# The first microseconds of a four-layer convolution stack: weight kernels loaded ahead of the input frames, weights computed while the frames arrive, and layer 1's weights made later

## The chip, the core and the metric

The kernel runs on one core of one Trainium2 chip. The metric is the device time of one launch in microseconds (us). The core has five engines with a queue of instructions each: PE (TensorE, the matmuls), DVE (VectorE), ACT (ScalarE), POOL (GpSimd) and SP (SyncE, which here only issues DMAs). An engine takes its queue in order, so an instruction that waits holds up all behind it. ACT also issues some DMAs; such an issue stands in ACT's queue like any other instruction (it is shown as ACTq, those of SP as SPq).

## What is computed

An image batch `x` of 4 x 16 x 512 x 512 floats goes through four layers, each `x = x + conv(gn(x))` with a group norm of 8 groups. What the change touches is layer 0, cut to what matters:

```python
def _denoise_block(x, w1, b1, w2, b2, w3, b3, a, b, c):
    trip = _triplets(x)                       # each frame with its two neighbours
    o = a * conv(trip, w1, b1, dil 1) + b * conv(trip, w2, b2, dil 2) + c * conv(trip, w3, b3, dil 4)
    return tanh(o)
...
y = _denoise_block(x, blk1...)                # 16 frames per image
z = _denoise_block(y, blk2...)
...
x = x + _L0_conv_ref(_gn(x), ...)
```

Layer 1 is a 3 x 3 convolution with integer weights, layer 2 a box blur, layer 3 a convolution in the Fourier domain. Layer 1's weights are brought into their layout during layer 0, and that step is moved too.

## The kernel before, in words

Layer 0 (class `Layer0`, L121) takes the frames of an image in groups of four. Each group passes through six **slots** (`slot`, L668): in slot `(n, p)` PE computes tile `p` of group `n`, 14 x 16 matmuls into one of two PSUM tiles (`products`, L513, the matmul at L525). The six tiles of a group use six combinations `v` of the frames, in the order `ORDER = (1, 2, 3, 4, 0, 5)`, each with its own weight tile `w[q]`. I call the tiles of the first group m0 to m5.

What goes into the combinations: a raw frame is scaled and shifted on ACT (`normalised`, L377 and the two edge copies L378 and L379), transposed on DVE (L405), and gets its upper and lower rims from a second small tile `ek`, made the same way from a `rim` load that serves four frames (`rims`, L382). The scale and the shift come from the group norm: `bn_stats` of each half of a frame on DVE (`frame_stats`, L266), one aggregation for two frames (L268), a sum across partitions on POOL and a square root on ACT (`finish_stats`, L229, and `rstd_bias`, L806, the root at L812). DVE then forms the combinations (`early`, `late`; L441 is the shared helper `stt`), and after a tile is done ACT or DVE takes it out of PSUM (`gather`, L536).

The order is written out by hand (`manual_schedule`): `run` first calls `first` (L270), then the slots from group -1 on, and each engine's queue holds its instructions in the order in which the Python calls made them. `first` does, in this order:

- twelve loads of half frames (frames 0 to 5 of image 0, `HELD = 6`, L202) on SP;
- `layer1_weights` (L867): two loads on ACT, a memset (L876) and six products (L881) on DVE, and the store of the result on ACT (L882);
- `frame_stats` of frames 0 and 1;
- `weights` (L153): loads of the parameters `l0_par` (L159) and of the expanded kernels `l0_t` (L161), both on ACT, the weighted sums and their combinations on DVE (L163 to L178), and two stores of the result to a scratch in DRAM on ACT (L181);
- `load_weights` (L194) for each of the six `q`: four loads of 32 partitions each from that scratch into `w[q]`, on ACT (L196), 24 in all;
- twenty rim loads (two rim tiles, L202) on SP;
- `frame_stats` of frames 2 to 5, then `finish_stats` for the first three channel groups.

The slots of group -1 make the five frames that the first group needs first (0, 1, 3, 2, 4, in this order) and its first two combinations. `rest_of_first` (L297) runs at the end of each early slot: it loads and measures frames 6 to 15, two per turn, and in slot (-1, 3) calls `take_biases` (L183: two small loads on ACT, six small operations on DVE). Later, `load_weights` is called in a slot whenever the next tile belongs to the other convolution.

DMAs are numbered onto eight completion semaphores in turn, whichever engine issues them. A DMA that would reuse a semaphore whose earlier DMA is still out waits on its issuing engine until that DMA has landed. In the order of before, loads on SP thus wait for loads and stores that ACT issued.

Of the kernel before, what the change touches and what calls it, by code (L numbers as in the profile page):

```python
# [13 lines left out]
F32 = mybir.dt.float32  # L14
AF = mybir.ActivationFunctionType
# [5 lines left out]
P = 128  # L21
# [7 lines left out]
PX = 32  # L29
# [8 lines left out]
HELD = 6  # L38
# [12 lines left out]
def shape_constants():  # L51
# [57 lines left out]
    k["c_lc"] = (v[g].reshape(P, NYB, 8).transpose(1, 0, 2)[..., None] * of).reshape(NYB, P, P)  # L109
    row = np.zeros((P, 2, n))  # L110
    row[g == 3, 0] = fold(first)
    row[g == 3, 1] = -fold(hk)
    k["c_bias_row"] = row
# [3 lines left out]
def scratch(pool, name, shape):  # L117
    return pool.tile(shape, F32, tag=name, name=name)


class Layer0:  # L121
# [12 lines left out]
    def __init__(self, k, ctx, x1):  # L134
        self.k, self.tc, self.nc, self.a, self.x1 = k, k.tc, k.nc, k.a, x1
        tc = self.tc
        self.pools = {}
        for name, bufs in (("frames", 1), ("w", 1), ("sum", 1), ("ra", 2), ("rb", 2), ("x", 6), ("ek", 1)):
            self.pools[name] = ctx.enter_context(tc.tile_pool(name=f"l0{name}", bufs=bufs))
        self.psum = ctx.enter_context(tc.tile_pool(name="l0ps", bufs=2, space=PSUM))  # L140
        self.mv = k.stats.tile([P, NBG, 2], F32, name="mv1")
        self.top = k.stats.tile([P, B, C, 2], F32, name="top1")
        self.low = k.stats.tile([P, B, C, 2], F32, name="low1")
        self.frame_is = k.load(k.stats, "c_frame_is")
        self.parity = k.load(k.stats, "c_parity")
        self.free = [
            self.pools["frames"].tile([P, KN], F32, name=f"frame{i}", tag=f"frame{i}") for i in range(NFRAMES)
        ]
        self.todo, self.gn = {}, {}
        self.marks, self.moves = [], None  # L150


    def weights(self):  # L153

        k, nc = self.k, self.nc
        n = NPB * PX // 2
        self.w_dram = scratch(k.dram, "l0w", [2, PX, NQ, 2 * n])
        par = k.small.tile([P, 6], F32, name="l0par", tag="l0par")
        nc.scalar.dma_start(par, self.a["l0_par"])  # L159
        t = self.free[0][:, 0 : 9 * n].rearrange("p (d n) -> p d n", d=3)  # L160
        nc.scalar.dma_start(t, self.a["l0_t"].rearrange("p (d n) -> p d n", d=3))  # L161
        sums = self.free[1][:, 0 : 3 * n]
        nc.vector.tensor_scalar_mul(sums, t[:, 0], par[:, 3:4])  # L163
        for d in (1, 2):
            self.stt(sums, t[:, d], par[:, 3 + d : 4 + d], sums)
        c = [sums[:, i * n : i * n + n] for i in range(3)]
        s, u = (self.free[1][:, i * n : i * n + n] for i in (3, 4))
        wq = self.free[2][:, 0 : NQ * n].rearrange("p (q n) -> p q n", q=NQ)
        nc.vector.tensor_add(s, c[0], c[2])
        for q, op in ((1, ALU.add), (2, ALU.subtract)):  # L170
            nc.vector.tensor_tensor(wq[:, q], s, c[1], op)
        nc.vector.tensor_scalar_mul(wq[:, 1:3], wq[:, 1:3], -1.0 / 6.0)
        nc.vector.tensor_scalar_mul(u, c[2], 1.0 / 6.0)
        self.stt(u, c[0], 1.0 / 24.0, u)
        for q, f in ((3, 1.0 / 12.0), (4, -1.0 / 12.0)):
            self.stt(wq[:, q], c[1], f, u)
        nc.vector.tensor_scalar_mul(wq[:, 0], c[0], 0.25)
        nc.vector.tensor_copy(wq[:, 5], c[2])  # L178
        to = self.w_dram.rearrange("b p q (e n) -> e (b p) q n", e=2)
        for half in range(2):  # L180
            nc.scalar.dma_start(to[half], wq[2 * PX * half : 2 * PX * half + 2 * PX])  # L181
# [10 lines left out]
                self.stt(o, par[:, d : d + 1], par[:, 3 + d : 4 + d], o)  # L192

    def load_weights(self, conv, q):  # L194
        for i in range(4):
            self.nc.scalar.dma_start(self.w[q][PX * i : PX * i + PX], self.w_dram[conv, :, q])  # L196


    def move(self, to, src, what="loads"):
# [70 lines left out]
    def first(self):  # L270

        self.mv0 = self.k.stats.tile([P, G, 2], F32, name="xmv0")
        self.held = {}
        for t in range(HELD):
            fr = self.free.pop()
            raws = [fr[:, 2 * W * h : 2 * W * h + 2 * W] for h in range(2)]
            for h in range(2):
                self.load_half(raws[h], 0, t, h)
            self.held[0, t] = fr, raws
        self.k.layer1_weights(self.free[3])  # L280
        for t in range(2):
            self.frame_stats(t, self.held[0, t][1])
        self.weights()
        for q in ORDER:
            self.load_weights(0, q)
        self.rims_ahead = {t0: self.load_rims(0, t0) for t0 in (0, 1)}
        for t in range(2, HELD):
            self.frame_stats(t, self.held[0, t][1])
        self.free.append(self.held.pop((0, HELD - 1))[0])
        self.finish_stats(0, self.mv0[:, 0 : HELD // 2])  # L290
        self.ahead = []

    def load_ahead(self, t):
# [3 lines left out]
    def rest_of_first(self, n, p):  # L297

        if (n, p) == (-1, 0):
            for t in (HELD, HELD + 1):  # L300
                self.load_ahead(t)
        if (n, p) == (-1, 3):
            self.take_biases()
        for _ in range(2 if (n, p) in ((-1, 5), (0, 0)) else 1 if n >= 0 else 0):
            if self.ahead:
                t, raws = self.ahead.pop(0)
                self.frame_stats(t, raws)
                self.load_ahead(t + 2)
                for lo, hi in ((2, 5), (5, G)):
                    if t == 2 * hi - 1:  # L310
                        self.finish_stats(0, self.mv0[:, lo:hi], lo)
# [67 lines left out]
        nc.scalar.copy(xp[:, :, W + 8 : W + 16], xp[:, :, W + 6 : W - 2 : -1])  # L379
        return xp.rearrange("p s (k j) -> p k s j", j=16)  # L380

    def rims(self, b, t0, raw):  # L382
        nc, k = self.nc, self.k
        ss = []
        for n in range(2):
            t = k.small.tile([P, 4], F32, name=f"rs_{b}_{t0}_{n}", tag="rs")
            nc.vector.tensor_mul(t, self.frame_is, self.gn[b][n][:, t0 : t0 + 4])
            o = k.small.tile([P, 1], F32, name=f"ro_{b}_{t0}_{n}", tag=f"ro{n}")
            nc.vector.tensor_reduce(o, t, AX.X, ALU.add)
            ss.append(o)  # L390
        xp = self.normalised(raw, ss[0], ss[1], f"r{b}_{t0}")
        ek = self.pools["ek"].tile([P, 33, PX], F32, name=f"ek_{b}_{t0}", tag="ek")
        nc.vector.transpose(ek, xp)
        return ek
# [392 lines left out]
class Kernel:  # L787
# [79 lines left out]
    def layer1_weights(self, t):  # L867

        nc = self.nc
        self.l1_wt = scratch(self.dram, "l1_wt", [P, 2, 4, 2, C])  # L870
        w = t[:, 0 : 9 * C].rearrange("p (h d c) -> p h d c", h=3, d=3)
        row = t[:, 9 * C : 9 * C + 2]
        wt = t[:, 256 : 256 + 16 * C].rearrange("p (a n y c) -> p a n y c", a=2, n=4, y=2)
        nc.scalar.dma_start(w, self.a["l1_w"])
        nc.scalar.dma_start(row, self.a["c_pair"])
        nc.vector.memset(wt, 0.0)  # L876
        for a, yo, dhs in ((0, 0, (0, 1)), (0, 1, (None, 0)), (1, 0, (2, None)), (1, 1, (1, 2))):
            o = wt[:, a, 0:3, yo, :]
            for y, d in enumerate(dhs):
                if d is not None:  # L880
                    nc.vector.scalar_tensor_tensor(o, w[:, d], row[:, y : y + 1], o, ALU.mult, ALU.add)  # L881
        nc.scalar.dma_start(self.l1_wt, wt)  # L882
# [176 lines left out]
    def layer2(self, x2, x3, sums, gn, l3):  # L1059
        tc, nc = self.tc, self.nc  # L1060
        res, under_way = [], []
        with ExitStack() as ctx:
# [87 lines left out]
            with tc.manual_schedule():  # L1150
                for i in range(3):
                    load(i)
                normal(0)
                first(0)
                normal(1)
                for i in range(n + 1):
                    if i + 3 < n:
                        load(i + 3)
                    if i + 1 < n:
                        first(i + 1)  # L1160
                    if i + 2 < n:
                        normal(i + 2)
                    if i > 0:
                        column_sums(i - 1)
                    if i < n:
                        second(i)
                    advance()
                    if i > C and i % C == 1 or i == n:
                        b = (i - 1) // C - (i < n)
                        res.append(self.group_stats(gps, self.stats, f"x3_{b}", mv[:, b], G))  # L1170
                        if b == 1:
                            under_way.append(self.edges(l3, 0, res, sums, tiles, *eps))
# [547 lines left out]
```

## Time and profile before

| | us |
|---|---|
| median of 3 runs | 5329.93 |
| lowest, highest of these | 5324.8, 5330.24 |
| the profiled execution | 5314.9 |
| its span, first to last instruction | 5313.1 |
| ACT busy in it | 2491.1 (47%) |
| POOL busy in it | 6.8 (0%) |
| share of PE, DVE and DMA in the chain that ended last | 89%, 6% and 2% |

The granted clock of TensorE was 0.982 over the span. The profile is one execution; its durations are sums and means over that one. A row of its timeline gives the start in us, the duration (for merged rows that of the whole stretch), the engine, the line, the operation, what it writes and reads, how many instructions were merged, and in brackets how long the engine had been idle before it and what ended that. A row with SPq or ACTq is a DMA issue, not the transfer. A row of the waits gives who waited for what, the sum in us, how many times, and the longest.

### The profile page before, as it was taken

What the parts mean: (1) busy time and instruction counts of PE and PEld (TensorE: products, weight loads), DVE (VectorE), ACT (ScalarE), POOL (GpSimd) and SP (SyncE); (2) the same over time, 40 slices, a digit from 0 to 9 for tenths busy, and PEclk for the clock granted to TensorE, in tenths of its full rate; (3) what the DMA queues carried; (4) which work ended last, traced back from release to release, by engine and by line L of the source; (5) the groups of instructions that cost most, each with busy time, mean ns of one, the idle gap of its engine ahead of it and who ended that gap; (6) DMA issues with size and microseconds to landing.
All of it is one profiled execution on the core that took longest, in us unless ns stands there. A gap on an engine that the chain in (4) does not pass through costs nothing.

```text
span 5313.1 us, 270477 instructions
## 1 busy us (share of the span) xinstructions
PE 5014.8 (94%) x125040; PEld 3651.4 (69%) x125040; DVE 4034.6 (76%) x4764; ACT 2491.1 (47%) x3954; POOL 6.8 (0%) x20
## 2 busy tenths in 40 slices
PE   4999998999999999989999789998999989999999
PEld 3676676766776856758766655566887867777776
DVE  7867989768988669987689855555555578888887
ACT  2543445533255533444122445554454446666665
POOL 0000000000000000000000000000000000000000
PEclk9999999999999999999999999999999989999999
DMA  5555554555545455543346377776666655555554
GB/s 170 170 145 157 144 156 148 161 148 137 143 152 169 139 160 137 150 134 117 103 128 153 126 222 231 234 238 202 225 222 199 214 158 143 144 149 148 143 143 121
DMA packets 445356, 861.49 MB, mean 162 GB/s; under 512 B 74304, under 2 KB 96704, under 8 KB 443968
## 3 DMA queue, kind: packets, MB, share of 16 engines
q1 hardware_dynamic: 415792, 797.68, 51.8%
q10 hardware_dynamic: 28432, 46.52, 2.7%
q8 instruction: 979, 16.04, 1.4%
q14 instruction: 153, 1.25, 0.1%
HBM read 503.87 MB, written 340.03 MB: 159 GB/s over the span
## 4 chain that ended last, share of the span: by engine, by line
PE 89%; DVE 6%; issue 2%; DMA 2%; ACT 1%; SPq 0%; ACTq 0%; POOL 0%; DVEq 0%; POOLq 0%
PE m L525 51%; PE l1p L975 10%; PE l2p L1082 8%; PE u L1550 4%; PE s L1491 4%; PE u L1491 4%; PE u L1513 2%; PE pt L1525 2%; DVE l2o L1122 2%; PE l2p L1133 1%; DVE st L1123 1%; DVE frame L441 0%; PE pr L1535 0%; ACT xp L377 0%; DVE zr L627 0%
## 5 line engine op out<-in xcount | busy, mean ns | idle before, releaser
L525 PE MATMUL m<-frame,l0w 32*32 32x512 f32 x86016 | 2856.1, 604 | 170.5 <-DVE frame L481 74.4
L525 PEld LDWEIGHTS m<-frame,l0w 32*32 32x32 f32 x86016 | 2073.7, 103 | 952.0 <-issue 363.1
L441 DVE SCALAR_TENSOR_TENSOR frame<-frame,frame 128x2376 f32<-128x2376 f32 x232 | 607.9, 2629 | 9.2 <-DMA xs<-in_x 0.8
L975 PE MATMUL l1p<-l1q,l_wt 32*32 32x512 f32 x12288 | 482.6, 600 | 61.3 <-DVE l1q L965 35.7
L975 PEld LDWEIGHTS l1p<-l1q,l_wt 32*32 32x32 f32 x12288 | 258.3, 103 | 231.6 <-issue 155.4
L1122 DVE TENSOR_TENSOR l2o<-l2x,l2p 128x512 f32<-128x512 f32 x256 | 172.7, 675 | 270.4 <-PE l2p L1082 270.4
L652 ACT ACTIVATE junk<-xb,neg 128x1024 f32<-128x1024 f32 x256 | 294.2, 1149 | 62.1 <-DMA l0w<-l0w 32.9
L1082 PEld LDWEIGHTS l2p<-k_c_band,l2y 128*128 128x128 f32 x2048 | 256.8, 190 | 76.0 <-issue 55.2
L1082 PE MATMUL l2p<-k_c_band,l2y 128*128 128x144 f32 (+1 forms) x2048 | 284.3, 292 | 6.1
L1082 PE MATMUL l2p<-k_c_band,l2n 128*128 128x144 f32 (+1 forms) x2048 | 272.5, 294 | 14.4 <-ACT l2n L1100 10.9
L1111 ACT COPY l2y<-l2p 128x512 f32<-128x512 f32 x256 | 149.9, 586 | 286.9 <-PE l2p L1082 286.9
L1082 PEld LDWEIGHTS l2p<-k_c_band,l2n 128*128 128x128 f32 x2048 | 265.8, 199 | 15.3 <-ACT l2n L1100 11.4
L992 DVE BATCH_NORM_STATS2 l1st<-l1o 128x6 f32<-128x512 f32 x256 | 158.2, 681 | 140.3 <-ACT l1o L990 140.3
L990 ACT ACTIVATE l1o<-l1p,k_l_bias,l_osc 128x1024 f32<-128x1024 f32 x128 | 147.2, 1201 | 240.1 <-PE l1p L975 234.2
L1550 PE MATMUL u<-k_c_hil,zt 128*128 128x128 f32 x2048 | 255.9, 278 | 0.0
L558 ACT COPY C<-m 128x1024 f32<-128x1024 f32 x64 | 61.6, 1014 | 405.9 <-PE m L525 317.6
L1550 PEld LDWEIGHTS u<-k_c_hil,zt 128*128 128x128 f32 x2048 | 238.4, 192 | 2.1 <-issue 0.8
L405 DVE STREAM_TRANSPOSE frame<-xp 128x1056 f32<-128x1056 f32 x128 | 162.8, 1282 | 90.5 <-ACT xp L379 90.4
L1526 ACT COPY zt<-pt 128x512 f32<-128x512 f32 x256 | 131.4, 599 | 207.8 <-PE pt L1525 207.8
L1456 DVE TENSOR_TENSOR xc<-l3n,k_c_tab 128x2048 f32<-128x2048 f32 x64 | 146.7, 2292 | 108.1 <-ACT l3n L1440 108.1
L1569 DVE SCALAR_TENSOR_TENSOR l3o<-u,l3t 128x256 f32<-128x256 f32 x512 | 192.3, 427 | 22.3 <-ACT l3t L1561 19.5
L975 PE MATMUL l1p<-l1x,l_wt 32*32 32x512 f32 x4088 | 196.7, 597 | 0.0
(309 smaller groups left out, 6376.9 us busy)
## 6 DMA issues: line engine op xcount, KB each, us to landing
y<-y SPq DMA_DIRECT2D x256, 264.0 KB
frame<-y SPq DMA_DIRECT2D x512, 132.0 KB
x<-l1o SPq DMA_DIRECT2D x256, 256.0 KB
l2x<-x SPq DMA_DIRECT2D x64, 1024.0 KB
x<-l2o SPq DMA_DIRECT2D x64, 1024.0 KB
l3x<-x SPq DMA_DIRECT2D x256, 256.0 KB
out<-l3o SPq DMA_DIRECT2D x256, 256.0 KB
l1x<-x SPq DMA_DIRECT2D x252, 256.0 KB
```

What stands on the lines that cost most here:

```text
L405: nc.vector.transpose(v[:, :, 4 + h : 68 : 2], xp)
L441: self.nc.vector.scalar_tensor_tensor(o, x, f, y, ALU.mult, ALU.add)
L525: ins = nc.tensor.matmul(ps[PX * j : PX * j + PX, i, :].rearrange("p (k r) -> p k r", r=64), w[rows, n], v[rows, k0 : k0 + 8, r0 : r0 + 64 ...
L652: nc.scalar.activation(junk, xs[h], f, bias=neg, accum_out=self.out_sums[n][:, 2 * t + h : 2 * t + h + 1])
L975: ins = nc.tensor.matmul(ps[32 * j : 32 * j + 32, b, :], wt[rows, a, d], qs[v % 3][rows, k, d : d + W] if d < 3 else raws[v][rows, k], sta ...
L992: nc.vector.bn_stats(st[b][:, u, :], o[:, b, :])
L1082: nc.tensor.matmul(ps[:, lo:hi], lhs[:, k, at : at + P], band[:, j : j + hi - lo], start=(k == 0), stop=(k == 3), skip_group_check=True,)
L1111: nc.scalar.copy(yts[i][:, wb, :], ps)
L1122: nc.vector.tensor_add(o[:, hb, :], xt[:, hb, :], ps)
L1491: nc.tensor.matmul(ps[b][32 * j : 32 * j + 32], f[rows, n, j, :], x[rows, j, :], start=(i == 0), stop=(i == 2 and tag == "s"), skip_group_ ...
L1550: nc.tensor.matmul(po[:, bass.ts(k, P)], zt[:, b, k ^ 1, :], hil[:, k, :], start=False, stop=(k == 3), skip_group_check=True,)
L1569: nc.vector.scalar_tensor_tensor(o[:, v].rearrange("p k u -> p u k"), po[:, HW:W].rearrange("p (u k) -> p u k", u=2), s, t.rearrange("p (u ...
```

## The change

It has six parts, all in `first` or in the slots up to (0, 1).

1. `weights` becomes a generator in two halves. The first half is called ahead of the frame loads: it issues the loads of `l0_par` and `l0_t`, now on SP, in front of the twelve frame loads. The second half, the DVE work and the two stores (still on ACT), is called directly after the frame loads, ahead of all `frame_stats`.
2. A one-element `Sqrt` on ACT, with a memset of its input on DVE, stands at the start. ACT's first table load is placed ahead of it.
3. The 24 loads of `load_weights` in `first` go to SP (`queue`, chosen by whether `now` is still None), behind the twenty rim loads. Later calls, in slots, stay on ACT.
4. The `frame_stats` of all six frames follow each other. The scales of the two rim tiles (`rim_scale`, four small DVE operations each, cut out of `rims`) are computed together right after `finish_stats`, where before the second four stood between the transposes of frames.
5. `take_biases` moves from slot (-1, 3) to (-1, 5): on ACT and on DVE it now stands behind frame 4 instead of ahead of frame 2.
6. `layer1_weights` becomes a generator too. Its two loads go to SP in slot (-1, 1); its memset, its six products and its store (on ACT) are done in slot (0, 1), in a tile of its own, ahead of that slot's `bn_stats`.

The operations, their shapes and their number are otherwise unchanged: DVE gets one instruction more (a memset of one column), ACT one activation more, and 28 DMA issues move from ACT to SP. In the built program f11, the last half-frame load on SP, waits for the semaphore of the first weight store, and the second rim load waits for that of the second store. From slot (0, 2) on the two programs stand in the same order on every engine and use the same semaphores.

```diff
     def weights(self):
...
-        nc.scalar.dma_start(par, self.a["l0_par"])
+        nc.sync.dma_start(par, self.a["l0_par"])
         t = self.free[0][:, 0 : 9 * n].rearrange("p (d n) -> p d n", d=3)
-        nc.scalar.dma_start(t, self.a["l0_t"].rearrange("p (d n) -> p d n", d=3))
+        nc.sync.dma_start(t, self.a["l0_t"].rearrange("p (d n) -> p d n", d=3))
+
+        warm = k.small.tile([P, 1], F32, name="warm", tag="l0warm")
+        nc.vector.memset(warm, 1.0)
+        nc.scalar.activation(warm, warm, AF.Sqrt)
+        yield
         sums = self.free[1][:, 0 : 3 * n]
...
     def load_weights(self, conv, q):
+        queue = self.nc.sync if self.now is None else self.nc.scalar
         for i in range(4):
-            self.nc.scalar.dma_start(self.w[q][PX * i : PX * i + PX], self.w_dram[conv, :, q])
+            queue.dma_start(self.w[q][PX * i : PX * i + PX], self.w_dram[conv, :, q])
...
         self.held = {}
+        weights = self.weights()
+        next(weights)
         for t in range(HELD):
             fr = self.free.pop()
             raws = [fr[:, 2 * W * h : 2 * W * h + 2 * W] for h in range(2)]
             for h in range(2):
                 self.load_half(raws[h], 0, t, h)
             self.held[0, t] = fr, raws
-        self.k.layer1_weights(self.free[3])
-        for t in range(2):
-            self.frame_stats(t, self.held[0, t][1])
-        self.weights()
+        next(weights, None)
+        self.rims_ahead = {t0: self.load_rims(0, t0) for t0 in (0, 1)}
         for q in ORDER:
             self.load_weights(0, q)
-        self.rims_ahead = {t0: self.load_rims(0, t0) for t0 in (0, 1)}
-        for t in range(2, HELD):
+        for t in range(HELD):
             self.frame_stats(t, self.held[0, t][1])
         self.free.append(self.held.pop((0, HELD - 1))[0])
         self.finish_stats(0, self.mv0[:, 0 : HELD // 2])
+        self.rim_scales = {t0: self.rim_scale(0, t0) for t0 in (0, 1)}
...
-        if (n, p) == (-1, 3):
+        if (n, p) == (-1, 5):
             self.take_biases()
+        if (n, p) == (-1, 1):
+            self.l1w = self.k.layer1_weights(self.pools["sum"].tile([P, 1024], F32, name="l1w_make", tag="E"))
+            next(self.l1w)
+        if (n, p) == (0, 1):
+            next(self.l1w, None)
...
+    def rims(self, b, t0, raw):
+        nc = self.nc
+        ss = (self.rim_scales.pop(t0) if b == 0 and t0 < 2 else None) or self.rim_scale(b, t0)
         xp = self.normalised(raw, ss[0], ss[1], f"r{b}_{t0}")
...
-        nc.scalar.dma_start(w, self.a["l1_w"])
-        nc.scalar.dma_start(row, self.a["c_pair"])
+        nc.sync.dma_start(w, self.a["l1_w"])
+        nc.sync.dma_start(row, self.a["c_pair"])
+        yield
         nc.vector.memset(wt, 0.0)
```

More of the change, by code (lines that the diff above doesn't have):

```diff
@@ L149, in __init__ @@
         self.todo, self.gn = {}, {}
-        self.marks, self.moves = [], None
+        self.marks, self.moves, self.now = [], None, None
     def weights(self):
@@ L380, in normalised, with rim_scale @@
         return xp.rearrange("p s (k j) -> p k s j", j=16)
-    def rims(self, b, t0, raw):
+    def rim_scale(self, b, t0):
         nc, k = self.nc, self.k
@@ L390, in rims @@
             ss.append(o)
+        return ss
+    def rims(self, b, t0, raw):
+        nc = self.nc
+        ss = (self.rim_scales.pop(t0) if b == 0 and t0 < 2 else None) or self.rim_scale(b, t0)
         xp = self.normalised(raw, ss[0], ss[1], f"r{b}_{t0}")
```

## The prediction

> **What bounds the kernel now.** I read the page first. PE is busy for 94% of the span and leads the chain that ended last with 89%; the first of its 40 slices is the exception, with a 4:
>
> ```profile
> PE 5014.8 (94%) x125040; PEld 3651.4 (69%) x125040; DVE 4034.6 (76%) x4764; ACT 2491.1 (47%) x3954; POOL 6.8 (0%) x20
> PE   4999998999999999989999789998999989999999
> ```
>
> So the beginning, in which PE has nothing to do, is added in full to what follows. The timeline of the first 200 us shows what the beginning consists of (start, duration, engine, line):
>
> ```profile
> 6.14 1.29 DVE L266 BATCH_NORM_STATS2 xst<-frame 128x6 f32<-128x512 f32 x2 [1.53 <-DMA frame<-in_x]
> 8.41 1.29 DVE L266 BATCH_NORM_STATS2 xst<-frame 128x6 f32<-128x512 f32 x2 [0.98 <-DMA frame<-in_x]
> ...
> 18.03 0.57 DVE L163 TENSOR_SCALAR frame<-frame,l0par 128x672 f32<-128x672 f32 x1 [4.11 <-DMA frame<-in_l_t]
> ...
> 23.72 4.84 DVE L266 BATCH_NORM_STATS2 xst<-frame 128x6 f32<-128x512 f32 x8
> 23.84 1.25 ACTq L181 DMA_DIRECT2D l0w<-frame  x2
> ...
> 29.14 14.32 ACTq L196 DMA_DIRECT2D l0w<-l0w  x24
> ...
> 34.10 0.17 DVE L242 COPY xmp<-xmv 128x3 f32<-128x3 f32 x1
> ...
> 36.34 0.17 DVE L810 TENSOR_SCALAR v_x<-var 128x3 f32<-128x3 f32 x1
> 43.50 1.28 ACT L812 ACT_TABLE_LOAD   x1 [43.50 <-DMA l0w<-l0w]
> 44.80 0.20 ACT L812 ACTIVATE s_x<-v_x 128x3 f32<-128x3 f32 x1
> ...
> 47.02 1.24 ACT L377 ACTIVATE xp_r<-rim,ro,ro 128x1024 f32<-128x1024 f32 x1 [2.02 <-DVE ro L389]
> ...
> 53.42 1.24 ACT L377 ACTIVATE xp_r<-rim,ro,ro 128x1024 f32<-128x1024 f32 x1 [1.44 <-DVE ro L389]
> ...
> 74.38 46.38 PE L525 MATMUL m<-frame,l0w 32*32 32x512 f32 x1344 [74.38 <-DVE frame L481]
> ```
>
> Three things are to be seen. DVE waits 4.11 us for the kernels `l0_t`, issued at 5.72 and landed 12.25 us later beside the frames. The variance is ready at 36.51 (36.34 + 0.17), but ACT is issuing 24 loads until 43.5 and then loads a table, so the root starts at 44.80: 8.3 us late. And ACT waits 1.44 us before the second rim tile.
>
> PE waits twice more soon after; the timeline from 118 to 160 us:
>
> ```profile
> 119.95 2.63 DVE L441 SCALAR_TENSOR_TENSOR frame<-frame,frame 128x2376 f32<-128x2376 f32 x1
> ...
> 122.68 29.44 PE L525 MATMUL m<-frame,l0w 32*32 32x512 f32 x896 [1.93 <-issue]
> ...
> 153.31 7.26 PE L525 MATMUL m<-frame,l0w 32*32 32x512 f32 x213 [1.18 <-issue]
> ```
>
> The view names no releaser, but m3 starts 0.10 us after DVE ends its combination (122.58), and m5 0.10 us after DVE has taken the last piece of m3 out of PSUM (153.21). By the table of stretches DVE is busy for 42.38 of the 46.39 us under m0 to m2 and for 32.10 of the next 32.54. **So DVE, not PE, sets the pace from 75 to 153 us**: a start of m0 that is earlier than DVE can follow is given back at m3.
>
> The waits of SP's queue up to 50 us show a fourth thing, the shared completion semaphores:
>
> ```profile
> SPq L202 <- DMA l0w<-l0w: 9.3, 6, 5.4
> ```
>
> Loads on SP stand still for DMAs of another kind.
>
> **The change part by part.**
>
> *Kernels ahead of frames (part 1).* SP issues its three constants until 2.06, `l0_par` takes 0.66 (its row on ACT), so `l0_t` is issued at about 2.75. When does it land? Nearest row: the first frame half, 512 KB, was issued at 2.10 and used at 6.14, 4.0 us. `l0_t` has 1008 KB; the further 0.51 MB at 285 to 420 GB/s (the rates of the slices from 3 to 13 us) take 1.2 to 1.8 us. That gives 8.0 to 8.6; I take 8.2. Here the Trainium skill speaks against the change: "DMA: Bandwidth & Descriptors", section "Issuing engines are not separate DMA queues", says that DMAs run on the same 16 engines and interleave, whichever engine started them, and that another queue saves only issue time. Read so, `l0_t` shares with the frames as it did before, takes its 12.25 us again and lands at 15.0. But the rows show frames that stood in SP's one queue landing one after the other (6.14, 8.41), not together; ahead in that queue `l0_t` should land first. I go by the row; the rule's 15.0 is a rival.
>
> DVE's weights took 23.72 - 18.03 = 5.69 us, so they end at 13.9. Then all six frames' statistics: two frames took 28.88 - 23.72 = 5.16 and 34.10 - 28.88 = 5.22, so six take 15.5, to 29.4. (The first two, and `layer1_weights`, were hidden under the wait for `l0_t`; now these 5.2 us are in the open, and are counted.) From there to the scales: the same steps later in the trace, with no table and a free ACT, take 94.69 to 98.64 = 3.95, and the first rim scale 47.02 - 46.37 = 0.65. **The first `xp_r` starts at 34.0 instead of 47.02: 13.0 us earlier.**
>
> *Root's table (part 2).* Its 1.28 us goes to the wait for data at the start: inside the 13.0. The skill's "ScalarE: Activation LUTs", section "What ACT_TABLE_LOAD costs", counts 2.66 with a drain; here the root started 0.02 us after the load's end, so nothing beyond 1.28 was to be had. By the page the first `xp_r` would start 14.4 us earlier.
>
> *Loads back on SP (part 3).* What covers them? f11, the last half-frame, waits for the first weight store. The stores are issued at 14.0 to 14.6. Before, both landed at 29.0, 5.2 us after the first issue, with the frames nearly done; now frames are in flight, so at worst they behave like `l0_t` did before (12.25 us). From both ends they land at 19.2 to 26.8; I take 23, since the frames drain on the way. f11 then lands at about 25 and DVE wants it at 27.8. Of the rims ten issues at 0.62 us follow: first tile issued at 29.2, landed at 32.6 (a rim load took 3.41 in the chain); wanted at 34.0. Second tile at 38.8; wanted at 34.0 + 51.98 - 47.02 = 39.0. Close, but covered; at the worst end it is 3.6 us late. Then 24 weight loads at 0.43: SP is free at 46, the first weights landed at 40; m0 wants them at 59. Frames 6 and 7 come after that, in use from 65. Without this cover they'd cost 10.3.
>
> *Rim scales (part 4).* The 1.44 us wait goes; the second pair's 0.62 lies under ACT's `xp_r`. Gain 1.44.
>
> *Biases (part 5).* They lay from 65.32 to 66.48 ahead of frame 2's transposes: m0 gains 1.16. But DVE does them before m3 either way: net nothing there. Their loads now wait on ACT behind frame 4 (about 56); behind them on SP, frames 8 and 9 are wanted only at 75.
>
> *Layer 1's weights (part 6).* Memset 0.27 and six products 1.42 now stand in DVE's full stretch before m3: about 1.7 us lost, in full. Bounds: 0 if they fell into ACT's waits there (1.65 and 0.2 at 108 to 112), 2 with queueing; the order puts them after those waits, so 1.7. ACT's store waits for them, ahead of frame 6's and 7's making; ACT has idle time there (4.5 us), so nothing.
>
> *Sum.* m0 starts at 74.38 - 13.0 - 1.44 - 1.16 = 58.8. m3 starts at 122.68 - 13.0 - 1.44 + 1.7 = 109.9, while m2 ends at 58.8 + 46.4 = 105.2: PE's wait there grows from 1.93 to 4.7. From there both programs stand alike, so all later events shift together by **12.7 us**. The profiled execution, 5314.9 with 1.8 outside its span, would be 5302.2. The median of the runs, 15.0 above that execution for reasons that the profile doesn't show, gives 5329.93 - 12.7 = 5317.2.
>
> **The rivals.**
>
> *`l0_t` shares with the frames.* For: it took 12.25 us before, and eight loads are soon in flight. Against: the frames' order of landing. Landing at 15.0 instead of 8.2 leaves 5.9 us: 5324.0.
>
> *The rims are late.* For: one semaphore's wait on a store stands ahead of all rims. At the worst end 3.6 us are lost, and f11's statistics with it perhaps 1: gain 8, 5322.
>
> *SP's queue decides, slower.* Place: the rim loads behind the second weight store. Price: one for one, once the first rim tile is later than its cover. It wipes out the gain when that tile lands at 32.6 + 1.4 + 12.7 = 46.7, a store landing at 37, and costs 0.2% at 48. Example: both stores starved until 50 give 5343. Against: only 5.8 MB of frames can be ahead of them, 14 us at the 420 GB/s seen.
>
> *No effect.* The gain is absorbed by later waits (PE waits 68.7 us up to 3300 us with no releaser named). Against: they repeat per image, long after the programs have become alike. 5329.
>
> **How the numbers follow.** Main case 0.62, `l0_t` late 0.13, rims late 0.15, no effect 0.06, slower 0.04. Predicted 5317.2. The range: low end `l0_t` at 7.2 (all at 420 GB/s, 1 us more), products hidden (1.7), and 2.7 us of the spread of runs (5.4): 5312. High end takes in both late rivals with 1 of spread: 5325. A measurement of this kernel can tell about 0.2%, 10.7 us, from no change; the main case lies just beyond, so a fifth of it and nearly all of the late cases fall within. Faster 0.52, same 0.44, slower 0.04.
>
> **What would show it.** `l0_t`'s first use near 8; the first `xp_r` near 34, with DVE's scale as its releaser, not a rim; m0 near 59; a PE wait of 4 to 5 us ahead of m3; m3 near 110 and m5 near 140.6. It is wrong if DVE starts weights near 15, if `xp_r` waits for DMA, or if m5's shift isn't found at the end of layer 0.

## The result, and the profile after

The changed kernel takes 5310.3 us, the median of 11 runs (5302.77 to 5323.7). Beside it on the same chip the kernel before took 5328.27 (11 runs, 5321.76 to 5343.11). The ratio is 0.9972, with a 95% interval from 0.9961 to 0.9983: **15 us faster, between 9 and 21** (1 less the ratio, times 5328; the medians are 18.0 apart). The forecast was 12.7 us faster. Its median, 5317.2, was counted from the 5329.93 of the first three runs; 5310.3 lies 1.7 us below the low end of the range, 5312. But the kernel before was itself 1.7 us faster in this timing than in those three runs: against 5329.93 the range is a ratio of 0.9966 to 0.9991 and the forecast 0.9976, and 0.9972 lies inside.

The profiled execution took 5313.62 us with a span of 5311.8, only 1.3 us less than that of before. So the span alone can't show this change; the beginning has to be read. First the page:

```profile
PE 5017.0 (94%) x125040; PEld 3644.6 (69%) x125040; DVE 4034.8 (76%) x4765; ACT 2490.1 (47%) x3955; POOL 6.9 (0%) x20
PE   5999998999999999989999799998999989999999
```

PE's first slice has gone from 4 to 5 and a later one from 8 to 9; the busy times differ by less than 7 us. The timeline of the kernel after, up to 113 us, line by line against that of before:

```profile
7.87 0.57 DVE L168 TENSOR_SCALAR frame<-frame,l0par 128x672 f32<-128x672 f32 x1 [7.02 <-DMA frame<-in_l_t]
...
13.68 1.25 ACTq L186 DMA_DIRECT2D l0w<-frame  x2
...
23.30 14.45 SPq L208 DMA_DIRECT2D rim<-in_x  x20
...
31.28 0.17 DVE L826 TENSOR_SCALAR v_x<-var 128x3 f32<-128x3 f32 x1
31.49 0.20 ACT L828 ACTIVATE s_x<-v_x 128x3 f32<-128x3 f32 x1 [29.27 <-DMA rim<-in_x]
...
33.52 0.16 DVE L400 TENSOR_REDUCE ro<-rs 128x1 f32<-128x4 f32 x1
...
34.88 1.24 ACT L388 ACTIVATE xp_r<-rim,ro,ro 128x1024 f32<-128x1024 f32 x1 [3.19 <-DMA rim<-in_x]
...
41.29 1.24 ACT L388 ACTIVATE xp_r<-rim,ro,ro 128x1024 f32<-128x1024 f32 x1 [1.45 <-DMA l0w<-l0w]
...
61.08 46.21 PE L541 MATMUL m<-frame,l0w 32*32 32x512 f32 x1344 [61.08 <-DVE frame L497]
...
101.09 1.42 DVE L898 SCALAR_TENSOR_TENSOR l1w_make<-l1w_make 128x48 f32<-128x48 f32 x6
...
112.30 48.28 PE L541 MATMUL m<-frame,l0w 32*32 32x512 f32 x1417 [5.01 <-issue]
```

DVE starts on the weights at 7.87 instead of 18.03, and the root at 31.49 instead of 44.80, 0.04 us after its variance (DVE L826 ends at 31.45; the DMA in the root's brackets is not what released it). But the first `xp_r` starts at 34.88, although its scales were there at 33.68 (33.52 + 0.16): it waits for its rim. The second waits 1.45 us. That label names the DMA whose semaphore came last, which is shared; the wait stands at a rim tile, and an experiment below shows what it is for. m0 starts 13.3 us earlier than before, m3 10.4 us. The root's delay is gone and the wait for `l0_t` is shorter; what is late next are the rims. SP's waits up to 50 us tell why:

```profile
SPq L208 <- DMA frame<-in_x: 8.2, 5, 2.9
SPq L208 <- DMA l0w<-frame: 7.7, 2, 6.7
```

For 7.7 us SP stood still until ACT's two weight stores had landed, 6.7 of it ahead of f11 and 1.0 ahead of the second rim load.

**Where the gain can be measured.** The two kernels were profiled again beside the experiments, which were run in three sets. The beginning of the kernel before repeats closely, that of the changed kernel within 1.4 us, the rest does not (starts, but for the wait and the span):

| us | before | before again | after | after, second set | after, third set |
|---|---|---|---|---|---|
| second `xp_r` | 53.42 | 53.30 | 41.29 | 39.89 | 40.44 |
| m0 | 74.38 | 74.27 | 61.08 | 59.69 | 60.23 |
| PE's wait ahead of m3 | 1.93 | 2.04 | 5.01 | 4.40 | 4.79 |
| m3 | 122.68 | 122.57 | 112.30 | 110.91 | 111.49 |
| last matmul of layer 0 | 3026.0 | 3032.9 | 3019.9 | 3011.2 | 3005.2 |
| last matmul of layer 1 | 3645.6 | 3667.2 | 3648.9 | 3625.1 | 3619.5 |
| span | 5313.1 | 5334.8 | 5311.8 | 5286.2 | 5281.0 |

Two profiles of the kernel before differ by 0.1 us at m3 and by 21.7 in the span. The stretch from layer 0's last matmul to layer 1's last takes from 613.9 to 634.3 us, and the longer ones are not those of one kernel. In the execution on the page, a lead of 10.4 us at m3 was one of 6.1 at the end of layer 0, and a lag of 3.3 at the end of layer 1, whose stretch took 629.0 us instead of 619.6. The experiments are therefore compared at m3; whether it reaches the end, only the runs' times can say.

### The profile page after: what moved, and what is told of

It reads as the page before. It is cut to its first block, busy times and chain, and to the rows that moved or that the text cites. A ratio compares the mean times of both kernels' runs of the same rounds, so it can differ in the third digit from the quotient of the medians.

```text
span 5311.8 us, 270483 instructions
## 1 busy us (share of the span) xinstructions
PE 5017.0 (94%) x125040; PEld 3644.6 (69%) x125040; DVE 4034.8 (76%) x4765; ACT 2490.1 (47%) x3955; POOL 6.9 (0%) x20
## 4 chain that ended last, share of the span: by engine, by line
PE 90%; DVE 5%; issue 3%; DMA 1%; ACT 1%; SPq 0%; ACTq 0%; POOL 0%; DVEq 0%; POOLq 0%
PE m L541 52%; PE l1p L992 10%; PE l2p L1099 8%; PE u L1567 4%; PE s L1508 4%; PE u L1508 4%; PE u L1530 2%; PE pt L1542 2%; DVE l2o L1139 2%; PE l2p L1150 1%; DVE st L1140 1%; PE pr L1552 0%; DVE frame L457 0%; SPq L208 0%; DMA l0w<-frame 0%
```

## The experiments

Each is the changed kernel with one edit, unless it says otherwise; all compute the whole output. The two kernels that were timed have several runs and an interval; the others have one profiled run each, of which the beginning is read.

**The kernel before, again** (`r_before`).

> The kernel before, profiled again, to see how far one execution stands for others. If the first 220 us are fixed by the program, m0 starts again at 74.4, m3 at 122.7 and the restart of PE in the second group at 218.8, each within 0.3 us, and the spread of 20 us between runs arises later: then the end of layer 0 (last matmul at 3026.0 in the first profile) and of layer 1 (3645.6) move by several us. If the beginning itself is noisy, m0 and m3 move by 1 us or more.

The beginning repeated: m0 at 74.27, m3 at 122.57 (0.11 us apart from the first profile). The time was 5336.57 beside 5334.53 for the same kernel in that set.

**The changed kernel, again, in the second set** (`r_after`).

> The changed kernel, profiled again. If the beginning is fixed by the program, xp_r starts again at 34.9, m0 at 61.1, m3 at 112.3 with 5.0 us of PE wait ahead of it and a granted clock of about 0.73 in the 9 us after, and PE restarts in the second group at 209.1, each within 0.3 us. If the 5 us gap trips the clock only by chance, the clock after m3 is 1.00 this time and the restart in the second group is not later for it. Ends of layers 0 and 1 may move by several us.

m3 came at 110.91, 11.66 us earlier than in `r_before`; the second `xp_r` waited 0.54 us where the first profile has 1.45. So it did not repeat within the 0.3 us that were expected. The rims' lateness is what changes most in the beginning from execution to execution. The time was 5287.95, beside 5292.46.

**Without the early table load** (`no_warm`). Part 2 undone:

```diff
-        warm = k.small.tile([P, 1], F32, name="warm", tag="l0warm")
-        nc.vector.memset(warm, 1.0)
-        nc.scalar.activation(warm, warm, AF.Sqrt)
```

> Part 2 undone alone: no small root at the start. Theory: in the changed order ACT has nothing to do between the two weight stores (issued by 14.9) and the root (31.5), and the table load stands ahead of the root without a wait of its own, so it runs under DVE's statistics; the first xp_r stays at 34.9 and m3 at 112.3, within 0.2. Rival, the part is needed: the load stands in the path, xp_r and m3 are 1.28 us later (113.6)[...].

Its timeline, the load and the root:

```profile
15.21 1.28 ACT L825 ACT_TABLE_LOAD   x1 [15.21 <-issue]
...
31.72 0.20 ACT L825 ACTIVATE s_x<-v_x 128x3 f32<-128x3 f32 x1 [15.23 <-DVE v_x L823]
```

The load doesn't wait for the root's operand. It ran as soon as ACT had issued its two stores, 15 us ahead of the root, under DVE's statistics. m3 came at 111.84, among the three of after. Part 2 is worth nothing here: the load cost time before only because 24 DMA issues stood ahead of it on ACT.

**Weight loads on ACT** (`weights_act`). Part 3 undone:

```diff
-        queue = self.nc.sync if self.now is None else self.nc.scalar
+        queue = self.nc.scalar
```

> Part 3 undone alone: the 24 weight loads of the beginning stand on ACT again, ahead of the root. Theory: they can't start before the stores have landed (22.8) and take about 14 us there, so ACT is free at 37 to 38, the first xp_r starts at about 40 instead of 34.9 and m3 at 116 to 118 instead of 112.3. Rival, the queue of these loads doesn't matter because the rims are late anyway: xp_r stays within 1 us of 34.9 and m3 of 112.3.

```profile
21.90 16.55 ACTq L202 DMA_DIRECT2D l0w<-l0w  x24
...
27.39 19.44 SPq L208 DMA_DIRECT2D rim<-in_x  x20
...
38.50 0.21 ACT L828 ACTIVATE s_x<-v_x 128x3 f32<-128x3 f32 x1 [36.28 <-DMA l0w<-l0w]
...
41.95 1.24 ACT L388 ACTIVATE xp_r<-rim,ro,ro 128x1024 f32<-128x1024 f32 x1 [3.25 <-DMA rim<-in_x]
...
50.19 1.24 ACT L388 ACTIVATE xp_r<-rim,ro,ro 128x1024 f32<-128x1024 f32 x1 [3.26 <-DMA rim<-in_x]
```

ACT issued until 38.45, and the root stood behind it, as before. The rims started 4.1 us later than in after, since SP's loads now waited for the semaphores of these loads too (9.1 us, six times), the first `xp_r` started 1.3 us after its scales (40.53 + 0.16), and the second waited 3.3 us. m3 came at 121.20, 3 to 5 us later than was expected of this run, since the rims got later too: of the 10.4 to 11.7 us that the change gains, only 1.4 were left. **Early kernels are worth almost nothing without part 3.**

**Kernels on ACT's queue** (`kernels_act`). `l0_par` and `l0_t` stay ahead, but ACT issues them:

```diff
-        nc.sync.dma_start(par, self.a["l0_par"])
+        nc.scalar.dma_start(par, self.a["l0_par"])
...
-        nc.sync.dma_start(t, self.a["l0_t"].rearrange("p (d n) -> p d n", d=3))
+        nc.scalar.dma_start(t, self.a["l0_t"].rearrange("p (d n) -> p d n", d=3))
```

> Half of part 1 undone: l0_par and l0_t are still ahead of the frames, but on ACT's queue, so they are issued at 0.7 to 1.7, some 1.4 us earlier than on SP. Theory, what matters is standing ahead in the frames' own queue: from another queue l0_t shares the engines with the frames and lands at 11 or later instead of 7.8; DVE's weights, all statistics and m3 move by 3 us (115.3). Rival, the queue only saves issue time and data flow in order of issue: l0_t lands at 6.5 to 7 and m3 is at 112.3 or up to 1 us earlier.

```profile
1.17 0.45 ACTq L161 DMA_DIRECT2D frame<-in_l_t  x1
...
2.09 13.45 SPq L208 DMA_DIRECT2D frame<-in_x  x12
...
6.83 0.57 DVE L168 TENSOR_SCALAR frame<-frame,l0par 128x672 f32<-128x672 f32 x1 [5.98 <-DMA frame<-in_l_t]
```

`l0_t` was not in the frames' queue, and landed 1.0 us earlier than from SP, 5.66 us after its issue (5.30 in after). It was issued 1.4 us earlier because SP had its constants to issue first. So being ahead in SP's own queue is not what brings it early. m3 came at 110.32, 1.5 us earlier than in `no_warm`, which ran in the same set.

**Kernels late, from either queue** (`kernels_late`, `kernels_mid`). In the first, ACT issues `l0_t` after three `Sqrt` of 1024 columns; in the second, SP issues it behind four half-frames (2.1 MB):

```diff
...
+        warm = self.free[3][:, 0:1024]
...
+        for _ in range(3):
+            nc.scalar.activation(warm, warm, AF.Sqrt)
+        nc.scalar.dma_start(par, self.a["l0_par"])
+        nc.scalar.dma_start(t, self.a["l0_t"].rearrange("p (d n) -> p d n", d=3))
```

```diff
-        next(weights)
         for t in range(HELD):
+            if t == 2:
+                next(weights)
```

> l0_par and l0_t on ACT, held back to about 6 us by three roots of 1024 columns ahead of them, so that they are issued when before's were, with SP's frames in flight; all else as changed. Theory after kernels_act: what counts is how many bytes were asked for earlier, whichever queue; with five or six half-frames ahead l0_t lands at 14 to 18, near before's 12 us after issue, and m3 moves with it by 6 to 10 us (118 to 121). Rival: before's late landing came from layer 1's small loads and store on ACT ahead of it, not from the frames; then l0_t lands within 6 us of its issue, at 12 or earlier, and m3 is at 116 or earlier.

> l0_par and l0_t on SP behind the first four half-frames instead of ahead of all; all else as changed. Theory, bytes go in order of issue: 2.1 MB are ahead, so l0_t lands 5 to 6 us later than ahead of all, at 13 to 14; the statistics follow the weights on DVE, so the scale, xp_r and m3 move by the same 5 to 6 us less what the rims' lateness hid (m3 at 115.5 to 117). Rival, the ring shares the engines evenly between what is in flight: l0_t lands at 16 or later and m3 is at 119 or later; or place doesn't matter: l0_t lands before 10 and m3 within 2 us of 112.

The timeline of `kernels_late`, then that of `kernels_mid`:

```profile
4.63 0.48 ACTq L165 DMA_DIRECT2D frame<-in_l_t  x1
...
14.86 0.57 DVE L168 TENSOR_SCALAR frame<-frame,l0par 128x672 f32<-128x672 f32 x1 [12.95 <-DMA frame<-in_l_t]
```

```profile
4.61 0.55 SPq L161 DMA_DIRECT2D frame<-in_l_t  x1
...
13.29 0.57 DVE L168 TENSOR_SCALAR frame<-frame,l0par 128x672 f32<-128x672 f32 x1 [12.45 <-DMA frame<-in_l_t]
```

Issued first, `l0_t` took 5.3 us (SP) or 5.7 (ACT). Issued at 4.6, it took 8.7 behind the four half-frames of its own queue, and 10.2 from ACT's, when SP had asked for six. What it waited for is seen in the bytes that `kernels_late` had moved by 10.1 us (q1 is SP's queue, q10 ACT's; packets, MB, share):

```profile
q1 hardware_dynamic: 1010, 2.15, 66.5%
q10 hardware_dynamic: 114, 0.00, 0.6%
```

Of the six half-frames about four had gone (2.10 MB), and nothing of `l0_t`, which ACT had asked for 5.5 us before. By the packets in the traces it began to move at 10.13 in `kernels_late` and at 9.78 in `kernels_mid`, after 2.16 and 2.04 MB of SP's queue, and then took 4.0 and 3.1 us. So the bytes asked for ahead of it decide, mostly, from either queue; the price of the other queue is at most 1.5 us here. This does not explain all of the old delay. In before `l0_t` was issued behind five half-frames (2.62 MB) and began at 11.85, when 2.63 MB of SP's queue had moved, but then took 5.4 us (4.9 in before, again). The store of layer 1's weights stood ahead of it in ACT's queue and moved from 8.96 to 12.28; whether it made `l0_t` later was not tried by itself.

At m3 these delays of 6.9 and 5.3 us (against the changed kernel's 7.96 on the same chip) cost 5.2 and 3.5 (116.64 and 115.03 against 111.49), each 1.7 to 1.8 less: when the statistics are later, the rims are in time. Even with these late kernels m3 is 5.9 and 7.5 us earlier than in `r_before`.

**Biases at their old place** (`bias_back`). Part 5 undone:

```diff
-        if (n, p) == (-1, 5):
+        if (n, p) == (-1, 3):
             self.take_biases()
```

> Part 5 undone alone: the biases stand ahead of frame 2 again. Theory, DVE sets m3 and not PE: m0 is 1.2 us later (62.2), m3 stays at 112.3 within 0.2, and PE's wait ahead of it shrinks from 5.0 to 3.8. Rival, PE sets the pace: m0 and m3 both 1.2 us later (113.5), the wait stays at 5.0.

From the second `xp_r` to m0 it is 20.96 us, in after 19.79: m0 gives up 1.17. To m3 it is 71.03, in after 71.01. PE's wait ahead of m3 shrank to 3.21 us. Nothing is lost at m3 (111.29), as only DVE counts there, and DVE does the biases on its way to m3 in both.

**Layer 1's weights in a hole of DVE** (`l1w_hole`). The memset and the six products of part 6 move from slot (0, 1) to the transposes of frame 5's rim tile, where DVE waited 1.65 us for ACT:

```diff
-        if (n, p) == (0, 1):
-            next(self.l1w, None)
...
         xp = self.normalised(raw, ss[0], ss[1], f"r{b}_{t0}")
+        if (b, t0) == (0, 5):
+            next(self.l1w, None)
```

> Layer 1's weights (memset and six products, 1.7 us of DVE) are moved from the end of slot (0, 1) to the place in that slot where DVE waits 1.65 us for the rim tile's xp_r. Theory: they fill that wait, m0 stays at 61.1, m3 comes 1.5 to 1.75 us earlier (110.6 to 110.8), and PE's wait ahead of it shrinks to 3.3 to 3.5 us. Rival, the products cost nothing where they are: m3 stays at 112.3. Whether a wait of 3.4 us still lowers the granted clock after m3 is open; if it doesn't, the clock there is 1.00 and m5 gains another 2 to 3 us.

From the second `xp_r` to m3 (109.73) it is 70.00: 1.0 us was won, not 1.7. DVE fell 0.7 us behind in the hole, and ACT's next `xp` waited 0.65 us for `l1w_make`.

**Weight stores behind the rims** (`stores_sp`). The two stores are issued by SP between the rims and the weight loads, so that no rim's semaphore is behind them:

```diff
+        yield
         for half in range(2):
-            nc.scalar.dma_start(to[half], wq[2 * PX * half : 2 * PX * half + 2 * PX])
+            nc.sync.dma_start(to[half], wq[2 * PX * half : 2 * PX * half + 2 * PX])
...
         self.rims_ahead = {t0: self.load_rims(0, t0) for t0 in (0, 1)}
+        next(weights, None)
```

> The two weight stores go to SP, behind the rim loads and ahead of the weight loads, so no load of a frame or a rim waits for a store. Theory, the rims were late only for that wait: f11 and the rims are issued from about 15 instead of 23.3, xp_r starts when the scale is ready, at 33.4 to 33.6 instead of 34.9, the second xp_r has no wait (38.4 instead of 41.3), m0 is at 58.2 and m3 at 109.4 (2.9 earlier). Rival, the rims are late because their 20 issues and transfers are slow in themselves: xp_r still waits for a rim load and m3 gains less than 1 us. A third way: the weights now come too late and m0 waits for them, later than 61.

```profile
15.08 17.42 SPq L209 DMA_DIRECT2D rim<-in_x  x20
...
33.91 1.24 ACT L390 ACTIVATE xp_r<-rim,ro,ro 128x1024 f32<-128x1024 f32 x1 [2.02 <-DVE ro L402]
...
38.78 1.24 ACT L390 ACTIVATE xp_r<-rim,ro,ro 128x1024 f32<-128x1024 f32 x1
```

The rims were issued 8.2 us earlier, the first `xp_r` was released by DVE, and the second did not wait. m3 came at 109.80. These are the numbers of the forecast (34.0, 39.0, 109.9), which had taken the rims as covered.

**All of it together** (`combo2`): `stores_sp`, `l1w_hole`, `kernels_act`, and the biases' loads on SP ahead of the rims with their six operations under frame 0's rim tile. **The changed kernel beside it** (`after_5`).

> All the changes that the runs before point to, on top of the changed kernel: l0_par and l0_t on ACT ahead of everything (landed 1.0 to 1.2 us earlier), the two weight stores on SP behind the rims (no rim waits for a store), the biases in DVE's wait for the first xp_r, layer 1's weights in DVE's wait for the third. Theory, DVE and ACT set m3, at the second xp_r plus 71.0 less what is taken from between (1.2 biases, 1.0 layer 1's weights): xp_r at 32.7, the second at 37.6, m0 at 57.4, m3 at 106.4, PE's wait ahead of it 3 us or less. Against the changed kernel (m3 at 111 to 112) that is 4.5 to 6 us, some 0.1% of the time; against the kernel before 15 to 17 us, ratio 0.997. Rival, the beginning's gain is lost again later: ratio to before as for the changed kernel or nearer to 1.

> The changed kernel beside combo2 on the same chip. Theory: 9.5 to 12 us less than before at the end of the first group and the same at the end, ratio 0.998; the 18 us between the medians of the first result hold 6 to 8 us of spread between runs. Rival, the changed kernel gains more later on than the beginning shows: ratio 0.9965 or less.

`combo2` reached m3 at 106.20, 5.3 us before the changed kernel's 111.49. Timed on one chip: `combo2` 5277.35 (9 runs, ratio to before 0.9968, 0.9956 to 0.9979), the changed kernel 5283.55 (11 runs, 0.9970, 0.9957 to 0.9984), before 5296.89 (19 runs). The medians are 6.2 us apart, near the 5.3 of the trace, but the intervals overlap almost wholly: that `combo2` beats the change in time isn't shown. The changed kernel's 0.9970 lies between what was expected of it, 0.998, and the rival's 0.9965, and its interval holds both.

## Why the prediction was right, and where it was off

**What sets m3.** The prediction said that DVE, not PE, sets the pace from 75 to 153 us. The runs show it as a constant: from the second `xp_r` to m3 it is 69.26 and 69.27 us in the two profiles of before, and 71.01 to 71.11 in ten of the changed order that left this stretch as it is, whenever the kernels landed and wherever the biases stood. The difference, 1.75, is the term for layer 1's weights, sized at 1.7. m3 is therefore the start of the second `xp_r` plus a constant, and the gain has to be found ahead of it.

**The kernels: right number, wrong reason.** Landing was put at 8.2 and came at 7.87 to 8.11 in the three profiles. But the step "ahead in that queue `l0_t` should land first" failed in `kernels_act`, where another queue did as well. The Trainium skill's "DMA: Bandwidth & Descriptors", section "Issuing engines are not separate DMA queues" (all queues run on the same 16 engines, another queue saves only issue time), agrees with that run. What failed was the reading of it as 15.0: issued ahead of all frames, from either queue, `l0_t` had little to share with: 0.2 to 0.35 MB of frames had moved by its last packet in the three profiles and in `kernels_act`. That the order of asking counts, whichever queue, is what the late pair shows.

**The root.** It starts at once, as forecast. Its saving was booked under part 2; `no_warm` shows that with part 3 it comes without part 2. Without part 3 the early load does save it: in `weights_act` the root starts 0.05 us after ACT's last issue, with no load between. `weights_act` also shows that 8.9 to 10.3 us of the whole gain at m3 need part 3.

**The rims: the step that was mis-sized.** "Close, but covered" was off by 1.0 to 2.6 us. The stores landed where they were taken to (f11 was let go at 22.9 to 23.0, 23 forecast). But the ten issues of the first rim tile ended at 31.08, 30.61 and 30.91, not at 29.2: the second of them stood another 1.0, 0.4 and 0.9 us for ACT's second store, which the prediction left out, and the rest followed each other every 0.67 us, not 0.62. So the first tile, landed by forecast at 32.6, was late: the first `xp_r` started 1.17 us later than its scales allowed in the first profile, 0.46 and 0.53 in the two others (0.03 us for the handover, seen in `stores_sp`, taken off). The second tile cost 1.45, 0.54 and 1.16. Together 2.6, 1.0 and 1.7, and m3 stood 2.4, 1.0 and 1.6 us behind the forecast 109.9. Not more than 0.2 us is left over. The prediction had named it as a sign of being wrong that "`xp_r` waits for DMA", and in all three profiles the first `xp_r` has a rim load as its releaser. This was the rival "the rims are late", whose 3.6 us were its worst end; it came true in part, by its own mechanism, and how much of it comes true changes from run to run: in `l1w_hole`, whose order is the same up to there, the first tile was in time and the second cost 1.02. `stores_sp` took the store ahead of the rims away, and with it both waits.

**The sum.** Forecast at m3: -13.0 - 1.44 + 1.7 = -12.7. Measured: the second `xp_r`, which holds the first two terms, is 12.1, 13.5 and 13.0 us earlier than the first profile of before, not 14.4, and 1.75 is given back: -10.4, -11.8 and -11.2. PE's wait ahead of m3 was put at 4.7 and came at 5.0, 4.4 and 4.8.

**The end.** The claim that later events shift together holds at m5: DVE's last piece out of m3, which m5 waits for, ends at 142.84 instead of 153.21 (10.37 earlier). It holds roughly in the second group, where PE next stops for DVE (before, then after):

```profile
198.81 15.53 PE L525 MATMUL m<-frame,l0w 32*32 32x512 f32 x448 [1.26 <-DVE frame L441]
189.18 15.24 PE L541 MATMUL m<-frame,l0w 32*32 32x512 f32 x448 [1.32 <-DVE frame L457]
```

That is 9.63 us earlier; the two other profiles of after have 186.85 and 187.57, the other of before 198.91. At the end of layer 0 it can't be read from single profiles, since the two of before differ there by 6.9 us. The runs' 15 us, 9 to 21, contain both the 12.7 and the 10.4 to 11.8, and rule out no effect and a loss. Whether the 3 to 5 us beyond the lead at m3 are real stays open: the second timing gave 16 us by its ratio, from 8 to 23, with medians 13.3 apart.

## What to carry to other kernels

A late load is brought forward by issuing it before the bytes that crowd it; which engine issues it matters little. When DMA issues move to another engine, look at the semaphores they share with their new neighbours: here a store held the loads behind it for 7.7 us. And measure a change of 0.3% at the first events behind it, where two profiles of the kernel before agreed within 0.1 us, not at the end of one profile, which moved by 21.7.

## What was not expected of the hardware

Where PE's wait ahead of m3 grew, its clock fell. The table of stretches, the 10 us after m3's start in after and in before (length; PE, PEld, DVE, ACT and POOL busy; granted clock, DMA share, GB/s):

```profile
112.30:122.30 10.00, 10.00 (x245) 6.25 (x256) 9.86 (x10) 3.52 (x8) 0.00 (x0) 0.75 0.49 127
```

```profile
122.68:132.68 10.00, 10.00 (x315) 7.03 (x324) 9.86 (x10) 3.56 (x9) 0.00 (x0) 1.00 0.63 157
```

In after 245 matmuls are recorded in 10 us, in before 315. The Trainium skill's "TensorE: Matmul & The Clock Gate", section "What's actually happening", gives half clock after an idle window of about 3.4 us. The traces agree on the half, but not on the wait: waits of 1.93 us (before) and 2.29 (`combo2`) left the clock at 1.00, one of 2.04 (the kernel before, again) saw 0.85 in the 10 us behind it, and waits of 3.2 to 5.9 us saw 0.71 to 0.84, in no order of their length. Cut finer, the clock around m3 is 0.50 for one stretch and 1.00 on both sides of it. The stretch in after, then in the kernel before, again:

```profile
110.50:117.33 6.83, 5.03 (x96) 2.31 (x97) 6.72 (x5) 2.43 (x4) 0.00 (x0) 0.50 0.74 169
```

```profile
122.22:125.63 3.41, 3.06 (x63) 1.47 (x65) 3.31 (x4) 0.28 (x1) 0.00 (x0) 0.50 1.02 231
```

In the twelve runs that have such a stretch it lasts 3.41 us (three runs) or 6.83, twice as long (nine). It begins 1.44 us (`no_warm`) to 4.92 us (`stores_sp`) after PE's stop, in two runs only after m3 had started. So the length of the wait alone decides neither when the clock falls nor for how long. It looks as if the clock were set at fixed steps of 3.41 us; that is read from these lengths, not tried.

It cost little. PE had waited 1.18 us for DVE ahead of m5 in before, and in after its matmuls run on from m3 through m5 in one row, without that wait. From m3 to PE's stop for DVE in the second group it is 76.13 and 76.34 us in the two profiles of before, and 76.88, 75.94 and 76.08 in the three of after: less than 1 us of the lead can have gone there.
